# Attention tiles: another order of key products and sums in TensorE's slot

## The chip, the cores and the metric

The kernel runs on one core of a Trainium2 chip. The metric is the device time of one execution in microseconds; of several runs the median is given. Five engines work in parallel, each through its own queue of instructions: TensorE (PE, its weight loads PEld), VectorE (DVE), ScalarE (ACT), GpSimd (POOL) and SyncE (SP, which issues transfers). They meet only at semaphores.

## What is computed

The input is 32 images of 128 channels and 56 x 56 pixels. Layer 0 is a 7 x 7 depthwise convolution, a layer norm and a mixture of 8 experts, top 2 of 8 per token. Layer 1 works on the 100352 tokens of 128 channels. Its attention looks at no other token: for each token and each of 8 heads of 16 channels it forms the 16 x 16 outer product of query and key, takes a softmax over the keys and multiplies by the values.

```python
attn = (q * scale)[..., :, None] * k[..., None, :]
attn = jax.nn.softmax(attn, axis=-1)
out = jnp.einsum('bhlij,bhlj->bhli', attn, v)
out = out.transpose(0, 2, 1, 3).reshape(B, L, C)
return out @ w_proj + b_proj
```

The result is added to the tokens; then comes an FFN in which each of 64 experts chooses 8 tokens of each image.

## The kernel before

The stages follow one another: convolution, routing, experts, attention (with the logits and the choice of the FFN in it), FFN and output. The change is in the attention stage, a loop over 784 tiles of 128 tokens (`while k < NT ...`, L1479). One pass of the loop is a slot, and in each slot the engines work on different tiles: `tile_work(k, back, what)` does step `what` for tile `k - back`, and a fourth argument of 2 lets it act on even tiles only, for two at once. The calls in the loop are the order of each engine's queue, because the wrapper `InOrder` (L153) ties each instruction to the one before it on its engine; all of its instructions carry line 161 in the profile. A group is 7 tiles, so there are 112 groups.

The steps of a tile, with the engine and the names in the profile:

- `keys` (L1091, TensorE, pairs of tiles): keys and values of two tiles into a PSUM bank, `kv<-wq,zT`. Three `kv` banks.
- `ends` (L1101, VectorE, pairs): largest and smallest key of each head, `kx<-kv`.
- `pivots` (L1108, GpSimd, pairs): the key that makes each score largest, `c`. It keeps the exponentials in range.
- `offsets` (L1128, VectorE): keys less pivot, spread over the queries, `s<-kv,c`, 128 x 2048.
- `scores` (L1137, GpSimd): times the query, `s<-s,q`.
- `exps` (L1145, ScalarE): `s<-s`.
- `values` (L1148, VectorE): exponentials times values, `ev<-s,kv`. It is the last reader of the `kv` bank.
- `sums_s` and `sums_ev` (L1161, L1166, TensorE): 16 accumulating transposes each, `sm<-ident,s` and `sm<-ident,ev`, for the denominators and numerators of the softmax. A bank `sm` holds both sums of two tiles; `sums_s` of an even tile takes a new bank, of two.
- `inverse_first` (L1169, ScalarE, pairs): `r<-sm` and `r<-r`, a first reciprocal of the denominators.
- `quotients` (L1174, VectorE, pairs): one refinement and the division, `sm<-sm,r`, `r<-sm,r`, `oT<-sm,r`. It is the last reader of the `sm` bank.

Beside the tiles runs the work on whole groups, cut into pieces with due places (`places`, L1432): two places in a slot, `group_work(2 * k)` and `group_work(2 * k + 1)`. It holds the layer norm of the next groups, their turning and queries (`p_x`, `p_q`), the projection of finished groups (`pp`), their turning (`p_u`), the FFN's logits (`p_l`, `p_g`), and `choose` (L1325), the choice of tokens for an image pair, in which VectorE has three instructions over 128 x 3136 (MAX8, MATCH_REPLACE8, and a SCALAR_TENSOR_TENSOR) and TensorE the pieces `cm` and `acc`. TensorE's pieces take a bank each, of three in turn with the tag `tp`, which ScalarE mostly reads and so frees. The eight banks of PSUM are thus 3 `kv`, 2 `sm` and 3 `tp`.

In an even slot TensorE's queue had: `keys` of tiles k+2 and k+3, `sums_ev` of tile k-3, group work, `sums_s` of tile k-2, group work. An odd slot had the same without `keys`.

Of the kernel before, what the change touches and what calls it, by code (L numbers as in the profile page):

```python
# [12 lines left out]
ALU = mybir.AluOpType  # L13
# [12 lines left out]
def conv_attn_hybrid_kernel(  # L26
# [392 lines left out]
    with tc.tile_pool(name="sel", bufs=1) as se, tc.tile_pool(  # L419
# [75 lines left out]
        for e in range(E):  # L495
            k = key[:, e, :]
# [181 lines left out]
    with tc.tile_pool(name="sc_c", bufs=1) as cc, tc.tile_pool(  # L678
# [51 lines left out]
        pe, ve, ac = (InOrder(e) for e in (nc.tensor, nc.vector, nc.scalar))  # L730
# [102 lines left out]
    with tc.tile_pool(name="ex_w", bufs=2) as ew, tc.tile_pool(  # L833
# [42 lines left out]
        for i, (e, b) in enumerate(blocks):  # L876
# [15 lines left out]
            xa, rows, n = got.pop(i)  # L892
# [60 lines left out]
    def fetch(i):  # L953

        e = slice(i * Q, (i + 1) * Q)
        fw1s[i] = big.tile([C, Q, FF2], F32, name="fw1", tag="s", bufs=5)
        nc.sync.dma_start(fw1s[i], weight1[e, :C, :].rearrange("e c f -> c e f"))
        fw2s[i] = big.tile([P, Q, NF2, C], F32, name="fw2", tag="ev", bufs=3)
        nc.sync.dma_start(fw2s[i], weight2[e, :FF2, :].rearrange("e (p f) o -> p e f o", f=NF2))

    with tc.tile_pool(name="at_c", bufs=1) as cc, tc.tile_pool(
# [56 lines left out]
        pe, ve, sc, gp = (InOrder(e) for e in (nc.tensor, nc.vector, nc.scalar, nc.gpsimd))  # L1018
# [45 lines left out]
        def heads(t):  # L1064
            return t.rearrange("p (h i) -> p h i", i=HD)

        def over_queries(t):
            return heads(t).rearrange("p h j -> p j h").unsqueeze(3).to_broadcast(sh)
# [19 lines left out]
        kvs, pivot, ss_, evs, sms, rs = ({} for _ in range(6))  # L1088
# [59 lines left out]
        def values(n):  # L1148
            ev = evs[n] = big.tile(sh, F32, name="ev", bufs=3)
            kv = kvs[n - n % 2][:, n % 2]  # L1150
            ve.tensor_tensor(ev, ss_[n], over_queries(kv[:, 1]), ALU.mult)

        def sums(t, out):

            for j in range(HD):
                pe.matmul(
                    out, t[:, j].rearrange("p h i -> p (h i)"), ident,
                    start=(j == 0), stop=(j == HD - 1), is_transpose=True,
                )

        def sums_s(n):  # L1161
            if n % 2 == 0:
                sms[n] = atp.tile([C, 2, 2, P], F32, name="sm")
            sums(ss_.pop(n), sms[n - n % 2][:, n % 2, 0, :])

        def sums_ev(n):  # L1166
            sums(evs.pop(n), sms[n - n % 2][:, n % 2, 1, :])
# [297 lines left out]
        def group_work(place):  # L1465
            for what, of in work.pop(place, ()):
                what(*of)
            if place in choices:
                choosing.append(choose(choices.pop(place)))
            if choosing and next(choosing[0], run) is run:  # L1470
                choosing.pop(0)

        def tile_work(k, back, what, every=1):
            n = k - back
            if 0 <= n < NT and n % every == 0:
                what(n)

        k = -22
        while k < NT or work or choosing or choices:  # L1479
            tile_work(k, 5, inverse_first, 2)  # L1480
            tile_work(k, -1, ends, 2)
            tile_work(k, 6, quotients, 2)
            tile_work(k, 0, offsets)
            tile_work(k, -1, pivots, 2)
            tile_work(k, 0, scores)
            tile_work(k, 1, exps)
            tile_work(k, -2, keys, 2)
            tile_work(k, 3, sums_ev)
            group_work(2 * k)
            tile_work(k, 2, values)  # L1490
            tile_work(k, 2, sums_s)
            group_work(2 * k + 1)
            if k == NT + 4:
                for i in range(3):
                    fetch(i)
            k += 1
# [121 lines left out]
```

## Time and profile before

| what | value |
|---|---|
| three runs | median 9425.73 us, 9423.46 to 9436.19 |
| profiled execution, its own time | 9417.63 us |
| its span | 9415.9 us |
| busy, whole span | PE 90%, PEld 72%, DVE 68%, ACT 56%, POOL 73% |
| attention's tile work | 4330 to 8864 us, 4534 us |
| one 128 x 2048 instruction | POOL 4605 ns, DVE 2281 and 2278, ACT 1915 |
| one of a sum's 16 matmuls | 276 ns, overlapping |

How to read it: a row of groups gives the instructions of one kind, their busy time and the mean of one; a row of waits says which engine's instruction sat idle for which other one, for how many us in all, how often, and the longest. A row of the timeline gives start, duration, engine and operation, then in brackets how long the engine had been idle and what ended that. Ends of matmuls are modelled, and neighbours overlap in the records, so that the start of the next is the better measure.

### The profile page before, as it was taken

The numbers are of one execution on the slowest core, as the hardware profiler recorded it, in microseconds if no ns is written. First come the engines' busy times: TensorE is split into PE (matmuls) and PEld (weight loads), VectorE is DVE, ScalarE is ACT, GpSimd is POOL, SyncE is SP. The second block draws the span as 40 slices with busy tenths as digits, with TensorE's granted clock in tenths as the row PEclk, the third lists the DMA queues.
The fourth block names the chain that finished last, engine by engine and source line by source line (L and its number), as shares of the span: only waits on it lengthen the run. The fifth ranks groups of instructions, "written<-read, shape, count | busy, mean of one in ns | idle before, by whom it ended". The sixth has DMA issues, their size and how long they took to land. (4 is left out here: it accounts for less than half of the span.)

```text
span 9415.9 us, 162622 instructions
## 1 busy us (share of the span) xinstructions
PE 8433.8 (90%) x60648; PEld 6763.7 (72%) x60648; DVE 6437.0 (68%) x10943; ACT 5265.5 (56%) x13401; POOL 6911.7 (73%) x5332
## 2 busy tenths in 40 slices
PE   9998278776999999997999999999999999999878
PEld 3436255554666666666888998988889989888733
DVE  2118889883222222226999999999999999999623
ACT  1118724332333333335888888888888888888600
POOL 0007267777777777778999999999999999999500
PEclk9999699998999999999999999999999999999855
DMA  9996157774444444441000000000000000000299
GB/s 210 215 204 179 34 171 225 209 209 121 69 67 72 65 61 70 70 68 32 25 31 32 30 30 32 25 32 32 28 32 32 25 32 30 30 32 32 65 323 335
DMA packets 996135, 849.73 MB, mean 90 GB/s; under 512 B 525012, under 2 KB 880663, under 8 KB 975858
## 3 DMA queue, kind: packets, MB, share of 16 engines
q1 hardware_dynamic: 470162, 494.25, 18.3%
q0 software_dynamic: 177664, 188.81, 11.3%
q10 hardware_dynamic: 347520, 156.28, 6.1%
q8 instruction: 480, 7.86, 0.3%
q14 instruction: 309, 2.53, 0.1%
HBM read 486.34 MB, written 353.64 MB: 89 GB/s over the span
## 5 line engine op out<-in xcount | busy, mean ns | idle before, releaser
L161 POOL TENSOR_TENSOR s<-s,q 128x2048 f32<-128x2048 f32 x784 | 3601.9, 4605 | 136.1 <-DVE s L161 105.5
L161 ACT ACTIVATE s<-s 128x2048 f32<-128x2048 f32 x784 | 1501.0, 1915 | 687.5 <-POOL s L161 684.0
L161 POOL DMA_INDIRECT t_d<-ys,xe x992 | 1530.6, 1543 | 406.1 <-issue 229.6
L161 DVE TENSOR_TENSOR s<-kv,c 128x2048 f32<-128x2048 f32 x784 | 1788.5, 2281 | 8.0 <-POOL c L161 8.0
L161 DVE TENSOR_TENSOR ev<-s,kv 128x2048 f32<-128x2048 f32 x784 | 1785.7, 2278 | 2.4 <-ACT s L161 2.4
L161 PE MATMUL sm<-ident,ev 128*128 128x128 f32 x12544 | 1531.9, 276 | 45.6 <-DVE ev L161 45.6
L161 PE MATMUL sm<-ident,s 128*128 128x128 f32 x12544 | 1526.3, 276 | 8.4 <-ACT s L161 8.4
L161 PEld LDWEIGHTS sm<-ident,ev 128*128 128x128 f32 x12544 | 1437.4, 144 | 92.9 <-DVE ev L161 50.8
L161 PEld LDWEIGHTS sm<-ident,s 128*128 128x128 f32 x12544 | 1404.8, 143 | 21.0 <-ACT s L161 8.9
L907 ACT ACTIVATE hT<-ph,b1t 128x512 f32<-128x512 f32 (+1 forms) x992 | 679.5, 685 | 1236.4 <-PE ph L903 1220.8
L918 DVE TENSOR_TENSOR ys<-py,b2t 128x512 f32<-128x512 f32 (+1 forms) x248 | 171.6, 692 | 1542.2 <-PE py L913 1445.5
L913 PEld LDWEIGHTS py<-w,hT 128*128 128x128 f32 x7936 | 959.3, 192 | 201.9 <-issue 91.4
L903 PE MATMUL ph<-xeT,w 128*128 128x512 f32 (+1 forms) x1984 | 921.6, 597 | 69.7 <-DVE xeT L899 69.7
L913 PE MATMUL py<-w,hT 128*128 128x128 f32 x7936 | 983.5, 278 | 0.2
L716 POOL DMA_INDIRECT xb_d<-xs,rd x784 | 765.3, 976 | 240.7 <-issue 202.0
L241 PE MATMUL cps<-xin,br 56*64 56x448 f32 x7168 | 684.4, 540 | 11.1 <-DVE br L235 10.7
L903 PEld LDWEIGHTS ph<-xeT,w 128*128 128x128 f32 x1984 | 348.7, 191 | 391.9 <-issue 293.1
L241 PEld LDWEIGHTS cps<-xin,br 56*64 56x64 f32 x7168 | 283.5, 132 | 411.2 <-issue 410.0
L161 PE MATMUL pa<-rw,ct 128*128 128x256 f32 x1568 | 395.4, 391 | 157.4 <-DVE xs L161 157.2
L287 POOL MEMSET code<- 128x64 f32 x1 | 0.2, 151 | 691.7 <-DMA conv_d<-ot 691.7
L161 PEld LDWEIGHTS pa<-rw,ct 128*128 128x128 f32 x1568 | 279.3, 191 | 290.8 <-DVE xs L161 209.2
L161 PE MATMUL kv<-wq,zT 128*128 128x256 f32 x1568 | 417.1, 389 | 54.5 <-DVE ev L161 54.1
(558 smaller groups left out, 13031.2 us busy)
## 6 DMA issues: line engine op xcount, KB each, us to landing
ct<-conv_d SPq DMA_DIRECT2D x192, 448.0 KB
xin<-in_x_dram SPq DMA_DIRECT2D x256, 196.0 KB
conv_d<-ot ACTq DMA_DIRECT2D x512, 98.0 KB
t_d<-xs ACTq DMA_DIRECT2D x112, 448.0 KB
tr<-t_d SPq DMA_DIRECT2D x112, 448.0 KB
to<-t_d SPq DMA_DIRECT2D x32, 1568.0 KB
out_dram<-oo ACTq DMA_DIRECT2D x32, 1568.0 KB
xg<-in_x_dram SPq DMA_DIRECT2D x96, 448.0 KB
```

The lines of the kernel that those rows point to most:

```text
L161: r = getattr(self.engine, name)(*a, **k)
L241: nc.tensor.matmul(pss[r][b * HP : (b + 1) * HP], br[rows, kw, :], xi[rows, b * NB : (b + 1) * NB, kw : kw + W], start=(kw == 0), stop=(kw ...
L287: nc.gpsimd.memset(code, -1.0)
L716: s = nc.gpsimd.indirect_dma_start(out=xb_d, out_offset=bass.IndirectOffsetOnAxis(ap=idx, axis=0), in_=row, in_offset=None, bounds_check=R ...
L903: nc.tensor.matmul(ph[:, :, :rows], w1[:, f * P : (f + 1) * P], xT[:, :, :rows], start=True, stop=True,)
L907: nc.scalar.activation(hT[:, f, :, :rows], ph[:, :, :rows], AF.Gelu, bias=b1t[:, f : f + 1])
L913: nc.tensor.matmul(py[:rows, j, :], hT[:, f, j, :rows], w2[:, f, :], start=(f == 0), stop=(f == NF - 1),)
L918: nc.vector.tensor_tensor(ys[:rows], py[:rows], across(b2t, SB)[:rows], ALU.add)
```

## The change

It reorders three calls in the loop. `sums_s` goes from behind `values` to ahead of `keys`, so it is TensorE's first work in a slot; `sums_ev` goes from ahead of the first place of group work to the place between the two places. As `sums_s` now stands ahead of `values` in the text, the dictionary entry of the tile's scores is removed in `values` and no longer in `sums_s`. In an even slot TensorE's queue then has: `sums_s` of tile k-2, `keys` of k+2 and k+3, group work, `sums_ev` of k-3, group work.

```diff
         def values(n):
             ev = evs[n] = big.tile(sh, F32, name="ev", bufs=3)
             kv = kvs[n - n % 2][:, n % 2]
-            ve.tensor_tensor(ev, ss_[n], over_queries(kv[:, 1]), ALU.mult)
+            ve.tensor_tensor(ev, ss_.pop(n), over_queries(kv[:, 1]), ALU.mult)
...
         def sums_s(n):
             if n % 2 == 0:
                 sms[n] = atp.tile([C, 2, 2, P], F32, name="sm")
-            sums(ss_.pop(n), sms[n - n % 2][:, n % 2, 0, :])
+            sums(ss_[n], sms[n - n % 2][:, n % 2, 0, :])
...
             tile_work(k, 0, scores)
             tile_work(k, 1, exps)
+            tile_work(k, 2, sums_s)
             tile_work(k, -2, keys, 2)
-            tile_work(k, 3, sums_ev)
             group_work(2 * k)
             tile_work(k, 2, values)
-            tile_work(k, 2, sums_s)
+            tile_work(k, 3, sums_ev)
             group_work(2 * k + 1)
```

## Prediction

> **What bounds the kernel now.** I read the busy shares by time first: the change lies in the attention stage, whose tile work runs from 4330 to 8864 us. Its row (busy us, counts in brackets):
>
> ```profile
> core 0: us, PE busy (x) PEld busy (x) DVE busy (x) ACT busy (x) POOL busy (x), PEclk, DMA share, GB/s
> 4330.00:8864.00 4534.00, 4300.97 (x35614) 4063.14 (x35613) 4374.10 (x3821) 3693.14 (x9151) 4269.43 (x2468) 0.98 0.09 30
> ```
>
> TensorE, VectorE and GpSimd are each busy 94 to 96% of 4534 us: 5.78 us for each of 784 tiles, and DMA is idle. No engine is the bound alone; what counts is who waits for whom. The waits of this stretch:
>
> ```profile
> DVE kx L161 <- PE kv L161: 110.9, 109, 14.0
> POOL s L161 <- DVE s L161: 105.5, 107, 3.5
> ACT r L161 <- PE sm L161: 84.2, 92, 2.2
> ...
> PE kv L161 <- DVE ev L161: 54.1, 27, 3.8
> ...
> PE sm L161 <- DVE ev L161: 45.6, 24, 3.5
> ...
> PE cm L161 <- ACT lg L161: 32.4, 22, 2.8
> ...
> PE cm L161 <- ACT sq L161: 18.3, 15, 1.5
> ```
>
> VectorE's only large wait is the first line: `ends` (L1105) waits for `keys` (L1096), 110.9 us. TensorE waits twice over: for VectorE's products (54.1 + 45.6) and, in group work, for ScalarE (the last two lines are its largest). So TensorE is sometimes too early, sometimes too late. The timelines show both. Too late, VectorE and then TensorE:
>
> ```profile
> 5630.91 0.76 DVE L161 TENSOR_REDUCE kx<-kv 128x16 f32<-128x256 f32 x2 [1.21 <-PE kv L161]
> 5631.58 2.28 DVE L161 TENSOR_TENSOR s<-kv,c 128x2048 f32<-128x2048 f32 x1
> ```
>
> ```profile
> 5629.84 1.03 PE L161 MATMUL kv<-wq,zT 128*128 128x256 f32 x4
> 5630.71 1.91 PE L161 MATMUL sm<-ident,ev 128*128 128x128 f32 x16
> 5632.46 0.49 PE L161 MATMUL p_x<-ident,zr 128*128 128x128 f32 x3
> 5632.78 1.91 PE L161 MATMUL sm<-ident,s 128*128 128x128 f32 x16
> ```
>
> The keys end at 5630.87 and `ends`, free to start at 5629.70, starts 0.04 us later. Too early, after `choose` has given VectorE a long instruction (TensorE's row):
>
> ```profile
> 5565.38 3.41 DVE L161 MATCH_REPLACE8 lg<-fm,lg 128x3136 f32<-128x3136 f32 x1
> 5568.70 2.28 DVE L161 TENSOR_TENSOR ev<-s,kv 128x2048 f32<-128x2048 f32 x1
> ```
>
> ```profile
> 5571.03 3.67 PE L161 MATMUL sm<-ident,ev 128*128 128x128 f32 x16 [3.51 <-DVE ev L161]
> ```
>
> **What the skill says.** "PSUM — Partial Sum Buffer", Engine vs sequencer instructions: the queues of ScalarE, VectorE and GpSimd are strict FIFO, and matmuls start in program order. So an early TensorE cannot pass a waiting piece; the 3.51 us agree. Same page, bank collisions: one engine may not read a bank that another writes, so waits go by bank, not address. The trace agrees: `inverse_first` reads only the exponentials' half of `sm`, yet in a quarter of the pairs it starts 0.04 us after the products' sums into that bank end. "Trainium Kernel Development and Optimization", Performance Expectations: judge TensorE by the weight loads' busy share; here 4063 / 4534 = 90%, so TensorE is full.
>
> **The change part by part.** No instruction is added or removed. The queues as built: TensorE's order changes as written; ScalarE's and GpSimd's are the same, VectorE's too but for numbering; on SyncE one FFN weight load at the stage's end goes three places sooner, at no cost where 30 GB/s move. Where the dictionary entry is popped (L1151, L1164) is bookkeeping. For a tile pair TensorE did keys, products, group work, exponentials, group work; products, group work, exponentials, group work. Now: exponentials, keys, group work, products, group work; exponentials, group work, products, group work. One 16-matmul sum takes TensorE 1.78 us (1.91 less its overlap with the next).
>
> I call lag the time from the end of `values` (which frees the `kv` bank) to the start of the next `keys`. VectorE then does `quotients` (they end 1.26 later), `offsets` and `values` (2.2 and 2.28; end 5.7 later), and then wants the keys, which take 1.03: a lag above 5.7 - 1.03, about 4.6, stalls VectorE by the rest.
>
> (a) Keys behind the exponentials. The sum opens a new `sm` bank, of two, so it waits for `quotients` (1.26 us after `values`). Least lag: before 0.05, after 1.26 + 0.05 + 1.78 = 3.1. The room between too early and too late shrinks from 4.6 to 1.5 us. Queued behind this new wait are keys and all group work; VectorE waits for the keys.
>
> (b) Products behind group work. The 45.6 us in which TensorE waited for products go: I set each such wait beside the exponentials of the next tile, and in all 21 that I could match they were done, so their sum fills it. This is a real gain.
>
> (c) Group work against ScalarE. At the same lag, every piece of group work now comes 1.78 us sooner after the keys, because one sum fewer lies between. Each piece takes one of three `tp` banks and waits until ScalarE has read the piece three before. I put each of 1478 pieces beside the end of that read: 147 start within 0.15 us of it (these wait already), 256 more within 1.78 us. Bounds: nothing, if ScalarE's reads move up too; at most 147 x 1.7 + 200 (what the 256 lack) = 450 us if each paid alone. Pieces of one pair share a delay, so it is less.
>
> (d) `inverse_first` waits for the products' sums, now later by the group work ahead, 0.79 us on average. ScalarE waits there already 84.2 us. Behind it are the exponentials, which `values` takes with at least 1.7 us to spare: nothing; if that cover went, up to 84 more waits of 0.8 = 65 us.
>
> The sum. I carried the lag through 370 pairs (4258 us) of this trace: lag, less the stall, plus TensorE's work to the next keys and its waits, less VectorE's work (each averages 11.28 us a pair; waits are taken out and put in by rule: products, quotients, banks). For the pair shown: lag 5.98, stall 1.21, left 4.77; plus 10.91, less 10.99, gives 4.69. The old order must return what was measured, and does:
>
> | us over 370 pairs | measured | carried, old | carried, new |
> |---|---|---|---|
> | TensorE waits for products or quotients ahead of sums or keys | 94 | 51 + 43 | 111 + 1 |
> | waits for exponentials | 0 | 0 | 3 |
> | waits for a `tp` bank | 110 | 107 | 231 |
> | VectorE stalls for keys | 97 | 95 | 237 |
>
> So (a) costs 60 and (b) gives 42, with 3 for exponentials; alone they leave VectorE 122 - 95 = 27 us worse. With (c) it is 237 - 95 = 142. The bank part, 115, holds ScalarE where it was; some of its reads wait for TensorE and would move up. I take three quarters of it, 86: 27 + 86 = 113, times 4534/4258 = 120 us for the stage. VectorE's stall is on the path: it delays `offsets`, and GpSimd starts a scores instruction right behind them (105.5 us of waits above). GpSimd has 4534 - 4269 = 265 us to spare and doesn't take over.
>
> Against the profiled execution's own time, 9417.6: 9538. The median of the three runs is 9425.7, 8.1 above it, so 9546.
>
> **The rivals.** Banks count little: ScalarE's idle time, nearly all in front of its exponentials, lets it read sooner. Then 27 x 1.065 = 29 us, 9455. For it: ScalarE is busy 81%. Against it: its group work stands behind exponentials that GpSimd sets.
>
> Faster: (b) alone decides. TensorE gains 43 us x 1.065 = 46, at the places where VectorE is late, and passes all of it on if it then reaches the heavy pairs ahead: 9380. This wins only if room lost in (a) is not used, that is, if after each long VectorE instruction the lag grows by less than 1.5 us. The pairs behind 5561.9 speak against it: from 0.05 the lag rises to 2.2, 4.2 and 5.9.
>
> No change: (a) and (b) cancel and banks are free: 9426.
>
> Worse: (c) in full with (d): 142 x 1.065 + 65 = 216, 9642.
>
> **How the numbers follow.** Banks count: 0.53, 9546. Banks little: 0.27, 9455. In full with (d): 0.06. No change: 0.07. Faster: 0.07. The likeliest is the prediction. A measurement of this kernel tells about 0.2% (19 us). Faster 0.07, within 0.07, slower 0.86. The range 9440 to 9615 leaves out faster, most of no change and the worst case, 0.19 together.
>
> **What would show it.** Right: VectorE's wait of `kx` for `kv` goes from 111 us to 200 or more; TensorE's waits for ScalarE in `cm`, `acc`, `p_x` double; its wait for `ev` nearly vanishes and one for `oT` (quotients) ahead of `sm<-ident,s` appears, over 100 us. Wrong: waits for ScalarE stay near 110 (then 9455), or `kx` waits less than 111 (then faster, and (a) is wrong); or `values` waits for exponentials, which (d) put at nothing.

## The result and the profile after

The changed kernel takes 9659.22 us (median of 4 runs, 9654.42 to 9665.19) where the kernel before, beside it, took 9430.06 (9423.46 to 9436.19): ratio 1.0246, interval 1.0234 to 1.0259. It is 229 us slower. I had forecast a loss of 120 us, with a range to 9615: the side was right, the size about half, and the time lies above the range.

Nearly all of the loss lies in the attention stage: between its first and its last `offsets` the two profiled executions took 4507.7 and 4741.8 us, 234 of the 248 us by which they differ. Its row in the busy times by stretch, as before (engines' busy us, clock, DMA):

```profile
4330.00:9094.00 4764.00, 4378.28 (x35570) 4122.01 (x35571) 4380.85 (x3818) 3684.72 (x9134) 4276.93 (x2466) 0.97 0.08 28
```

In these windows the stage takes 4764 us instead of 4534; VectorE, ScalarE and GpSimd are as busy as before, and TensorE, with the same instructions, is busy 77 us longer at a clock of 0.97 instead of 0.98. The waits of this stretch (who for whom, us, times, longest):

```profile
ACT r L161 <- PE sm L161: 595.1, 264, 4.8
ACT s L161 <- POOL s L161: 438.2, 269, 6.5
DVE kx L161 <- PE kv L161: 281.9, 224, 12.8
POOL s L161 <- DVE s L161: 212.9, 251, 5.3
PE sm L161 <- DVE oT L161: 120.3, 39, 4.1
...
PE acc L161 <- ACT sq L161: 69.9, 29, 2.7
...
DVE sm L161 <- ACT r L161: 64.0, 22, 4.0
...
PE cm L161 <- ACT lg L161: 28.2, 21, 2.6
...
PE cm L161 <- ACT sq L161: 24.2, 15, 1.8
```

Two lines of the kernel before, for comparison:

```profile
DVE sm L161 <- ACT r L161: 17.0, 19, 7.1
...
PE acc L161 <- ACT sq L161: 15.3, 19, 2.1
```

VectorE's wait for keys rose from 110.9 to 281.9 us, TensorE's wait for products gave way to one for quotients (`oT`, 120.3), and `acc` waits longer for ScalarE. These I had named; but `cm`, named too, waits as before (28.2 + 24.2 us, where it was 32.4 + 18.3). The first line I had not named: `inverse_first` waits for the sums 595.1 us, where it was 84.2, and the quotients then wait 64.0 for it instead of 17.0.

### The profile page after: what moved, and what is told of

Read it like the earlier page. It is cut to its first block, busy times and chain, and to the rows that moved or that the text cites. A ratio compares the mean times of both kernels' runs of the same rounds, so it can differ in the third digit from the quotient of the medians.

```text
span 9663.5 us, 162808 instructions
## 1 busy us (share of the span) xinstructions
PE 8526.5 (88%) x60648; PEld 6820.8 (71%) x60648; DVE 6451.0 (67%) x10943; ACT 5262.9 (54%) x13401; POOL 6921.8 (72%) x5332
## 5 line engine op out<-in xcount | busy, mean ns | idle before, releaser
L161 PE MATMUL sm<-ident,s 128*128 128x128 f32 x12544 | 1540.0, 277 | 139.5 <-DVE oT L161 120.3
L161 PE MATMUL sm<-ident,ev 128*128 128x128 f32 x12544 | 1556.5, 279 | 0.4
L161 PEld LDWEIGHTS sm<-ident,s 128*128 128x128 f32 x12544 | 1429.1, 144 | 153.7 <-issue 105.4
L161 DVE TENSOR_REDUCE kx<-kv 128x16 f32<-128x256 f32 x784 | 294.9, 418 | 283.6 <-PE kv L161 281.9
```

The lines of the kernel that those rows point to most:

```text
L161: r = getattr(self.engine, name)(*a, **k)
```

## The experiments

Two theories. **Theory A**: the products' sums come late, `inverse_first`, which shares their bank, waits for them, and in ScalarE's queue it holds up the exponentials and the group work whose reads free TensorE's banks. **Theories B and C** are my prediction's steps: TensorE has less room because keys stand behind a sum (B), and its group work comes sooner after keys and meets occupied banks wherever ScalarE is (C). Each time below is set against the kernel before, measured beside it (medians of 9424 to 9429 us).

**e1 and e2: `inverse_first` behind the exponentials**, in the changed kernel and, as a control, in the one before.

```diff
-            tile_work(k, 5, inverse_first, 2)
...
             tile_work(k, 1, exps)
+            tile_work(k, 5, inverse_first, 2)
```

> The changed kernel with inverse_first moved behind the exponentials in ScalarE's slot; all else as changed. Theory A (late products' sums hold up inverse_first, which holds up the exponentials and all of ScalarE's group work behind it, which frees TensorE's banks late): ScalarE's wait of r for sm falls from 595 us to below 150, the quotients' wait for r from 64 to below 20, TensorE's waits for ScalarE in group work from 228 towards 150; time about 9580 (9425 plus the 151 us that the ledger gave with ScalarE left where it was). Theory B (only TensorE's smaller room, keys behind a sum and group work sooner after keys; ScalarE's lateness is a follower): no change, 9640 to 9670.

> Control: the kernel before with the same move of inverse_first behind the exponentials. Theory A: the 84 us wait of r for sm falls below 20, little else was lost to it, so 9400 to 9426. Theory B: no change, 9426 within 10. A slowdown would mean that the move itself costs (r later for the quotients), and then the first run is to be read with that cost taken off.

Measured: e1 9599.75 (ratio 1.0185, 1.0168 to 1.0202), e2 9500.99 (1.0083, 1.0066 to 1.01). The wait of `r` for `sm` went from 595 to 43 us in e1, but the quotients' wait for `r` stayed at 60.5 us, which theory A had below 20. And the control lost 76 us, against both theories: the quotients waited 150 us for the later `r`. So the move has a price of its own, and e1's gain of 59 only shows the direction. Another edit had to take the wait away.

**e3: keys first, only the products late. e4: exponentials first, products at once.** Both from the changed kernel:

```diff
-            tile_work(k, 2, sums_s)
             tile_work(k, -2, keys, 2)
+            tile_work(k, 2, sums_s)
             group_work(2 * k)
```

```diff
             tile_work(k, -2, keys, 2)
+            tile_work(k, 3, sums_ev)
             group_work(2 * k)
             tile_work(k, 2, values)
-            tile_work(k, 3, sums_ev)
```

> The changed order with keys ahead of the sums of exponentials again: keys, exponentials, group work, products, group work. Keys come as soon as values free their bank, and group work stands behind keys and one sum, as before; only the products' sums are later than before, now by one sum and the group work. Theory A: ScalarE's wait of r for sm stays at 500 us or more and the time at 9600 to 9720. Theory B: the room is back, VectorE's wait for keys falls to about 110 us, time 9420 to 9450.

> Exponentials first, then keys, then products, then both places of group work one behind the other: keys stand behind a sum as in the changed kernel, and the products' sums follow keys at once as before. Theory A: r waits about 84 us, and what is left is the smaller room, 27 to 80 us: 9455 to 9510. Theory B: most of the cost stays, 9550 or more, with TensorE waiting about 100 us for quotients and VectorE over 200 us for keys.

Measured: e3 9570.93 (1.0152, 1.0135 to 1.0169), e4 9476.48 (1.0055, 1.0039 to 1.0072). Theory B wanted e3 back at 9420 to 9450; it loses 146, less than the 9600 or more of theory A. VectorE's wait for keys is nearly the old one there, and the others are A's:

```profile
ACT r L161 <- PE sm L161: 686.9, 298, 4.9
...
DVE kx L161 <- PE kv L161: 128.9, 142, 3.7
DVE sm L161 <- ACT r L161: 126.6, 125, 5.4
```

e4 lies where A put it, +51. So there are two costs, and neither theory has both.

**e5 and e6: `inverse_first` waits for nothing.** It computes from a constant tile `given`, filled once, which leaves the true denominators out of the first reciprocal; number, size and order of the instructions in the loop stay.

```diff
-            sc.activation(r, sms[n][:, :, 0, :], AF.Ln)
+            sc.activation(r, given, AF.Ln)
```

> The changed kernel, with inverse_first computing from a constant tile in SBUF instead of the denominators in PSUM (this leaves the true denominators out of the first reciprocal, so the softmax is not computed; the instructions and their sizes stay). It then waits for no sum at all. Theory A (inverse_first waits for the late products' sums and holds up ScalarE): only the cost of exponentials ahead of keys is left, 9465 to 9510; ScalarE's wait of r for sm is gone, quotients no longer wait for r, TensorE's waits for ScalarE in group work fall from 228 to 110 to 150. Theory C (these waits come from group work being 1.78 us sooner after keys, wherever ScalarE is): they stay above 190 and the time above 9560.

> Control: the kernel before with the same constant for inverse_first (the softmax is not computed here either). Both theories: nearly nothing, since r waited 84 us for sm and only 17 us reached VectorE: 9400 to 9426, waits of group work for ScalarE 90 to 115.

Measured: e5 9552.31 (1.0138, 1.0118 to 1.0158), e6 9429.54 (1.0002, 0.9993 to 1.001). The control is free this time. So the wait of `inverse_first` costs the changed kernel 229 - 128 = 101 us, give or take some 20 by the intervals, and 128 are left: more than theory A allowed (9510), less than theory C wanted (above 9560). In e5 the line of `r` for `sm` is gone and the quotients wait 5.7 us; what remains:

```profile
DVE kx L161 <- PE kv L161: 229.9, 208, 13.7
PE sm L161 <- DVE oT L161: 113.6, 45, 3.5
...
PE acc L161 <- ACT sq L161: 38.2, 30, 2.2
PE p_g L161 <- ACT sq L161: 31.2, 29, 1.4
```

**e7: the products later still**, behind both places of group work.

```diff
             group_work(2 * k)
             tile_work(k, 2, values)
-            tile_work(k, 3, sums_ev)
             group_work(2 * k + 1)
+            tile_work(k, 3, sums_ev)
```

> A dose: as the changed kernel, but the products' sums behind both places of group work: exponentials, keys, group work, group work, products. Theory A: inverse_first waits still longer, r for sm 750 us or more, quotients for r 100 or more, time 9720 to 9850. Theory C: the group work of the second place comes still one sum sooner, 9680 to 9720, with the quotients' wait for r as in the changed kernel.

Measured: 9941.97 (1.054, 1.0517 to 1.0564), worse than either theory's range. `r` waits 1040.0 us, VectorE 541.7 for keys, and TensorE's waits for ScalarE in group work are 473 us where they were 228; but the quotients wait for `r` only 53, where theory A wanted 100 or more. In this order the wait of `inverse_first` and the waits in group work grow together, and no run with the constant tile tells them apart.

**e9 and e10: e3 and e4 with `inverse_first` on the constant tile**.

> Keys, exponentials, group work, products, group work (as the third run), with inverse_first on a constant tile (the softmax is not computed). No room is lost, group work stands behind keys and one sum as before, and inverse_first waits for nothing: only that the products are later by themselves is left. If the 146 us of the third run were all the wait of inverse_first: 9420 to 9445, waits of group work for ScalarE 110 to 130. If late products cost by another way, or the group work is held up by itself: above 9480.

> Exponentials, keys, products, group work, group work (as the fourth run), with inverse_first on a constant tile (the softmax is not computed). inverse_first cost little there (r waits 187 us for sm, quotients 6 for r), so 9460 to 9480: the price of keys behind a sum that waits for quotients. If it falls to 9435 or below, the fourth run too paid for inverse_first and not for the room.

Measured: e9 9422.27 (0.9996, 0.9987 to 1.0004), e10 9467.31 (1.0043, 1.0029 to 1.0057). e9 settles one cost: e3's 146 us were all the wait of `inverse_first`. Its waits are those of the kernel before:

```profile
DVE kx L161 <- PE kv L161: 107.9, 117, 14.1
PE kv L161 <- DVE ev L161: 71.1, 38, 3.4
PE cm L161 <- ACT lg L161: 48.1, 22, 5.0
```

From e9 to e5 only keys and one sum change places, and that costs some 130 us. In e10, too, keys stand behind this sum, but group work of the first place still follows the products; that costs 39. From e10 to e5 only the products and the first place of group work change places, and that costs the other 89: the products' later place cost nothing in e9, but in e5 this group work follows keys at once.

**e11 and e12: the exponentials' sums one slot later**, so that the sum ahead of keys takes a bank that was free long before. e11 is e5 with this, e12 is e4 with it.

```diff
-            tile_work(k, 2, sums_s)
+            tile_work(k, 3, sums_s)
             tile_work(k, -2, keys, 2)
```

> The changed order with inverse_first on a constant tile (the softmax is not computed) and with the exponentials' sums one slot later, so that the sum ahead of keys opens its bank a whole slot after the quotients that free it. Group work is as soon after keys as in the changed kernel. If the lost room (the wait for quotients, 114 us in the fifth run) costs what the fourth run says: about 50 less than the fifth run's 9552, so 9490 to 9515, and TensorE's wait for oT is gone. If the sooner group work is the whole cost and the wait for quotients is only where TensorE would have waited for products anyway: 9540 to 9560.

> A proposal, with the whole computation: exponentials of the tile one slot later first, then keys, products, both places of group work. No sum waits for quotients, products follow keys at once, and TensorE has a sum to do while values are late. By the account of room and inverse_first together: the fourth run's 9476 less most of its 51 us, and less up to 40 for waits that the sum fills: 9390 to 9435. If instead the second place of group work being sooner after keys is what the fourth run paid for: 9460 to 9480.

Measured: e11 9554.74 (1.013, 1.0113 to 1.0146), e12 9482.99 (1.0055, 1.0038 to 1.0072): the same as e5 and e4, so e12 misses the gain that it was proposed for. In e11:

```profile
DVE kx L161 <- PE kv L161: 237.2, 192, 13.0
PE cm L161 <- ACT lg L161: 68.6, 22, 5.0
PE p_x L161 <- ACT sq L161: 49.9, 22, 4.0
...
PE kv L161 <- DVE ev L161: 37.2, 15, 3.8
```

The wait for quotients, 113.6 us in e5, is gone; part of it came back as waits for products (57 in all), and the waits in group work rose from 168 to 245. TensorE came earlier and stood at the next gate, that is, the next place where its queue waits. So the lost room (B), as a wait for quotients, is not a cost by itself.

**e13, e14, e15: an early release of the `p_u` banks**, in e5, in the changed kernel and in the one before. The squares are taken from the copy in SBUF.

```diff
-                squares(ps[:, j - j0, :], ss[:, j : j + 1])
+                squares(u[:, j, :], ss[:, j : j + 1])
```

> The fifth run (changed order, inverse_first on a constant tile, softmax not computed), and the squares of tail_rows are taken from the copy u in SBUF instead of the bank p_u, so that the bank is free after one copy and not after four more pairs of instructions. ScalarE's instructions stay the same in number. If the 127 us that the fifth run still loses are waits for banks: the 107 us of waits that ended with sq fall below 40, the time by 50 or more, to 9440 to 9500. If keys behind a sum cost in another way: 9540 to 9560, and the waits move to another place.

> The changed kernel with the whole computation and the same early release of the p_u banks. The waits of TensorE that ended with sq, about 150 us, fall to below 60; the wait of inverse_first stays at 400 us or more. If banks carry a part of both causes: 9540 to 9600. If not: 9640 to 9665.

> Control: the kernel before with the early release. Its waits that ended with sq are about 56 us of 113; if banks cost there too, up to 50 us are won: 9375 to 9415. If nothing: 9426.

Measured: e13 9566.39 (1.0151, 1.0134 to 1.0168), e14 9619.74 (1.0208, 1.0191 to 1.0225), e15 9438.83 (1.0014, 1.0007 to 1.0021). In e13 no wait ended with `sq` any more, but the waits in group work were 175 us instead of 168: they ended with `lg`, the reader of the next bank. The time is no better. This doesn't tell whether banks carry e5's 128 us: the edit moved the wait and did not shorten it. In e14 the waits in group work fell by 23 us, the quotients' wait for `r` by 30, and the loss from 229 to 194, between the two forecasts. The control lost 13 instead of gaining; why is open. e13's 14 us above e5 are about this price, so the early release gained nothing there, while in e14 it gained 35 in spite of it.

**e8 and e16: the other direction.** From the kernel before: in odd slots the next keys, and the products that `inverse_first` waits for, go ahead of the last group work; e16 adds the early release.

```diff
-            tile_work(k, -2, keys, 2)
-            tile_work(k, 3, sums_ev)
+            if k % 2:
+                tile_work(k, 3, sums_ev)
             group_work(2 * k)
             tile_work(k, 2, values)
             tile_work(k, 2, sums_s)
+            tile_work(k, -3, keys, 2)
+            if k % 2:
+                tile_work(k, 2, sums_ev)
             group_work(2 * k + 1)
```

> A proposal in the other direction, from the kernel before: in the odd slot the keys of the next pair and the products' sums that inverse_first waits for are put ahead of the last group work instead of behind it. Least lag of keys is still 0.05 us, group work comes one piece later after keys. Theory A: r for sm waits less than 84 us and TensorE's waits for ScalarE fall below 100, VectorE's wait for keys below 100: 9380 to 9420. If it is slower, something sets keys early that my account lacks.

> The eighth run (keys and the products behind them ahead of the last group work) with the early release, the whole computation: its waits that ended with sq, about 54 us, go. If both add: 9365 to 9410.

Measured: e8 9414.73 (0.9988, 0.9982 to 0.9995), e16 9426.78 (1.0001, 0.9992 to 1.001). e8, with the whole computation, is ahead of both kernels, by 10 us of 9424; e16 is not, as one expects when the 13 us that the early release cost in e15 are added. In e8 `r` hardly waits for `sm` (10 us), VectorE waits a little less for keys, but TensorE waits more for products (it was 54.1) and ScalarE for TensorE's group work (10.1):

```profile
DVE kx L161 <- PE kv L161: 101.3, 100, 13.1
...
ACT ls L161 <- PE p_l L161: 91.4, 54, 2.8
...
PE kv L161 <- DVE ev L161: 73.1, 37, 4.2
```

## Why the prediction was too small

All 740 tiles from tile 20 to 760, summed from the traces by who ended the wait (waits over 0.1 us); the second column is the account of the prediction, over as many tiles:

| us over 740 tiles | before | carried, new order | changed | e5 | e10 | e9 |
|---|---|---|---|---|---|---|
| TensorE waits for products or quotients | 94 | 112 | 120 | 114 | 117 | 85 |
| TensorE waits for ScalarE in group work | 113 | 231 | 228 | 168 | 115 | 123 |
| all idle time of TensorE | 208 | 346 | 354 | 282 | 232 | 209 |
| TensorE busy | 4063 | taken as 4063 | 4140 | 4112 | 4095 | 4063 |
| TensorE at half clock | 133 | not in it | 280 | 225 | 188 | 123 |
| VectorE waits for keys | 96 | 237 | 259 | 215 | 152 | 94 |
| quotients wait for `r` | 9 | taken as 9 | 57 | 5 | 6 | 9 |
| time of the 740 tiles | 4271.4 | | 4493.7 | 4394.2 | 4326.9 | 4271.5 |

**(d) failed: "nothing".** It was the step for the products' delay of `inverse_first`, and this costs 101 us (changed less e5), or 152 in the order of e3 (e3 less e9). The delay itself was mis-sized. I put it at the group work ahead, 0.79 us, and left out that in an even slot the exponentials' sum, 1.78 us, now also stands ahead of the products that `inverse_first` waits for. From the start of ScalarE's exponentials in that slot to the end of these products the trace has 3.13 us on average before and 5.66 in the changed kernel: 2.5 us more. There were 264 waits, 2.3 us each on average. In e4, with 4.13 us, the wait costs 13 us (e4 less e10), which is within the noise.

The path was missed too. I looked only at `values`, which did not wait for exponentials, and bounded the rest at 65 us. By the waits, the loss reaches VectorE in two ways: the quotients take `r`, 57 - 5 = 52 us; and ScalarE's group work stands behind `inverse_first` and frees the banks late, 228 - 168 = 60 us of TensorE's waits, after which VectorE waits 259 - 215 = 44 us longer for keys. 52 and 44 are nearly all of the 99 us between e5's tiles and those of the changed kernel.

**(c) had the right total for partly the wrong reason.** With ScalarE held where it was, the account said 231 us of bank waits, and 228 came. But without the wait of `inverse_first` there are 168. Sooner group work raises them by 55 and not by 124; late reads add the rest. I had taken three quarters, because ScalarE would "move up". e5 fits that, and less than a half came; in the changed kernel ScalarE moved back instead.

**(a) is not a wait for quotients.** That wait came as sized (120 against 111), but e11 shows that without it TensorE waits elsewhere and the time stays. e10's 39 us are the price of keys behind a sum, together with the second place of group work, which there comes one sum sooner. **(b) was right**: the waits for products are gone.

**(a) to (c) together** cost 128 us in e5, near the 120 of the forecast, and in near parts: 39 and 89, where I had 29 for (a) with (b) and 92 for (c). (The profiled execution of e10 was 10 us above its median and that of e5 9 below, so the tiles in the table show 56 and 67.) This is in part luck: waits for ScalarE in group work rose by 55 where I took 86, and 49 us of longer TensorE time, which the account did not have, fill the rest. That (c) carries the 89 is argued from the order of the calls and from these waits, 53 us more in e5 than in e10; no run changed the banks alone.

**TensorE's work was held constant, and it isn't.** It grew by 77 us, a third of the loss. Two views of the changed kernel show how at one place, TensorE's timeline and the clock by stretch:

```profile
4737.95 0.66 PE L161 MATMUL p_x<-ident,zr 128*128 128x128 f32 x4 [1.07 <-ACT sq L161]
4741.67 3.65 PE L161 MATMUL sm<-ident,s 128*128 128x128 f32 x16 [3.07 <-DVE oT L161]
4745.11 1.92 PE L161 MATMUL kv<-wq,zT 128*128 128x256 f32 x4
...
4748.08 1.97 PE L161 MATMUL sm<-ident,ev 128*128 128x128 f32 x16
```

```profile
4736.00:4741.00 5.00, 1.53 (x13) 1.06 (x10) 4.96 (x4) 4.21 (x25) 4.92 (x3) 0.95 0.48 201
4741.00:4748.00 7.00, 6.33 (x30) 5.67 (x30) 5.82 (x7) 3.99 (x8) 6.85 (x2) 0.55 0.20 86
4748.00:4753.00 5.00, 4.23 (x39) 3.90 (x37) 4.97 (x4) 2.89 (x5) 4.69 (x5) 1.00 0.01 3
```

After a wait of 3.07 us the sum takes 3.65 us instead of 1.91 and the keys 1.92 instead of 1.03, at a granted clock of 0.55 (third value from the right). The keys stand behind the sum that waits, so it is they that come late.

What stays open: how e5's 128 us divide between occupied banks, half clock and the keys' own later place. TensorE idles 74 us more there than before and is busy 49 us longer; e10 parts the orders, but no run took one of these causes away alone.

## What to carry to other kernels

Before a step is moved on one engine, list who waits for it by its bank and not only by its data, and then what is queued behind that waiter: here a small ScalarE instruction, 0.8 us a pair, carried 101 us. When a step moves, count everything that then stands ahead of it in the slot: here one sum was forgotten, and the delay was 2.5 us instead of 0.8. In this loop, in which three engines are at least 94% busy, a wait that was taken away reappeared at the next gate (e11, e13), so only a time decides, not a line of waits. A control with the same edit on the kernel before is needed: e2 showed that the first remedy cost 76 us by itself.

## What the runs showed of the hardware

TensorE's clock fell to half in this stage for stretches of 3.4 or 6.8 us (in the kernel before also one of 10.2). Over the 740 tiles of the table it did so 28 times in the kernel before, 133 us in all, and 59 times, 280 us, in the changed one. The Trainium skill, "TensorE: Matmul & The Clock Gate", HAM oscillation, tells of idle gaps of more than some 3.4 us. The lengths agree with its window, the threshold does not: the largest gap near a fall was 2.7 us at the median in the changed kernel and 1.7 at the least. In the 3.4 us ahead of a fall TensorE was idle there for 65% of the time at the median and 51% at the least (38% in e5).

So a wait on a nearly full TensorE can cost more than its length: its busy time grew by 77 us beside 146 us of added idle time. At half clock the sum above took about twice as long, so the added 147 us at half clock can account for at most 73 of the 77, and the added 92 in e5 for 46 of its 49. In e9, with 10 us less at half clock than before, TensorE is busy as long as before.
